# End of layer 0 by image: squares in the scan, attention from the sums of the projection's input, results applied from PSUM

## The chip, the cores and the metric

The kernel runs on one core of a Trainium2 chip. The metric is the device time of one execution in microseconds (us). The program is one launch of about 147,000 instructions on five engines: PE (matmul and, as PEld, its weight loads), DVE (vector), ACT (scalar), POOL (GpSimd) and SP (which here issues DMAs). Each engine works through its own queue of instructions in a fixed order that the framework lays down when the program is built; engines wait for one another with semaphores.

## The reference: what is computed

Four layers run one after the other on an image tensor x of 4 images, 256 channels and 32x32 = 1024 positions (tokens). Layer 0 is a state-space mixer (Mamba-2) with channel attention, layer 1 a non-local block with batch norm, layer 2 attention and a mixture of experts, layer 3 attention and an LSTM of 1024 steps. Everything is float32. The change lies in the end of layer 0, which the reference writes so:

```
y = ys + Dp * xs                                  # output of the scan, per token 256 values
y = y * silu(z)
y = y * rsqrt(mean(y * y, axis=-1) + EPS) * rms_w # RMS norm of each token over its 256 values
out = einsum('bld,ed->ble', y, out_w)             # projection 256 -> 256
out_img = out.transpose to (b, c, h, w)
pooled = mean(out_img over h, w)                  # one number per image and channel
hdn  = relu(pooled @ se1_w.T + se1_b)             # 256 -> 64
attn = sigmoid(hdn @ se2_w.T + se2_b)             # 64 -> 256
x = x + out_img * attn                            # per image and channel
```

Since the projection is linear, the mean of the projected tokens of an image is the projection of the mean of its tokens. The changed kernel uses that.

## The kernel before

The tensor `x` stays in SBUF for the whole program as `s.x`, with channels on the partitions: 2 chunks of 128 channels (`C`), 4 images (`B`), 1024 tokens (`L`). Tokens are handled in tiles of 128 (`NT` = 32 tiles, `TPI` = 8 per image) and in blocks of 512 (`NBLK` = 8 blocks, `BPI` = 2 per image, `TPB` = 4 tiles per block). `_layer0` (L219) normalizes, projects and convolves image by image, computes the decays of the recurrence (`_decays`, L331), and then calls `_scan` (L376) and `_out_and_se` (L439).

`_scan` runs 32 iterations: 8 chunks of 128 tokens outside, 4 images inside, so that all four images end together in the last four iterations. An iteration transposes the inputs on PE into the PSUM tile `ptr` (L395), copies them to SBUF on ACT (`xb`, L398), takes the exponential of the decays on ACT (`m_h`, L409), multiplies on DVE and POOL (L400 to L433), and ends with one DVE multiplication by the gate into `zs[:, n, :]` (L436). ACT has two instructions in an iteration. The scan's PSUM pool holds four names with two buffers each, which is all eight banks.

`_out_and_se` then treats all 32 token tiles together. It squares every tile on ACT and sums along the tokens' 256 values (`sq`, L449), takes one square root over all sums on ACT (L451) and a reciprocal on DVE (L452). Then it goes through the 8 blocks: scale four tiles by `rstd` on DVE (L459), transpose them on PE into `pt`, two chunks of channels of four tiles each (L463), evict `pt` to `yT` on DVE with the multiplication by `rms_w` (L464), project on PE into `po` (L470), and evict `po` to the SBUF tile `o` on ACT, which also sums over the tokens (L473). After the last block follow the two small matmuls of the channel attention for all images (L484, L489), its relu and sigmoid on ACT (L486, L491), and eight DVE instructions of 1024 elements that multiply `o` by the attention and add it to `s.x` (L493). Layer 1 (L499) starts with six small DVE instructions (`theta_wide` and its like, L510) and then matmuls over all of `s.x` (L521).

Who sets the order: the framework's scheduler takes the instructions of the source, and gives each engine an order from priorities (earlier in the source comes first) and from a model of when inputs and buffers are ready; on DVE the instructions of neighbouring iterations of the scan are interleaved in the trace. A tile pool has a number of buffers for each name; when a pool is closed, its memory is given to pools that open later, which then wait until the earlier users are done.

A helper that the change uses exists already: `_rsqrt` (L911) computes 1/sqrt(v + EPS) on DVE alone, by an integer first guess and four Newton steps, sixteen small instructions in all. It is written as a generator, so that callers can mix its steps with others.

## Time and profile before

| | us |
|---|---|
| median of 3 runs | 3567.6 (3564.02 to 3568.08) |
| the profiled execution's own time | 3564.65 |
| its span, first to last instruction | 3562.9 |
| last instruction of the scan (L436) ends | 295.19 |
| first matmul of the output projection (L470) starts | 312.88 |
| last projected block is evicted (L473) | 354.45 |
| first addition to `s.x` (L493) starts | 357.28 |
| first matmul of layer 1 (L521) starts | 367.28 |

The profile gives times from the start of the span. From the end of the scan to the first matmul of layer 1 is 367.28 - 295.19 = 72.1 us, which is 2% of the span. In a view of stretches each row holds, for every engine, its busy us in the stretch and in brackets the number of instructions. In a view of groups each row holds the line of the kernel, the engine, the operation, the tiles it writes and reads, their shapes and the number of instructions; then the busy us and the mean ns of one; and then the time for which the engine stood idle just before these instructions, with what ended it. A float32 matmul shows as two PE records.

### The profile page before, as it was taken

The page shows a single profiled execution, that of the slowest core. Times are in us where ns is not written, and L with a number is a line of the kernel's source. Part 1 is how long each engine was busy: PE and PEld are TensorE (multiplying, and loading weights), DVE is VectorE, ACT ScalarE, POOL GpSimd, SP SyncE. Part 2 cuts the span into 40 slices and gives each one's busy share as a digit, 9 for nine tenths or more (in the row PEclk, how much of TensorE's full clock was granted, in tenths as well). Part 3 has the DMA queues.
Part 4 walks back from the last instruction along what each step waited for, and adds up shares of the span by engine and source line. Part 5 has one row for each costly group of instructions (what it writes and reads, how often), then busy time and mean ns, then how long its engine had stood idle before and what let it go on. Part 6 is the DMA issues. An engine that isn't in the chain of part 4 may idle for free.

```text
span 3562.9 us, 146932 instructions
## 1 busy us (share of the span) xinstructions
PE 3253.3 (91%) x65426; PEld 2549.0 (72%) x65426; DVE 2028.1 (57%) x8373; ACT 1249.5 (35%) x5057; POOL 416.0 (12%) x498
## 2 busy tenths in 40 slices
PE   7786599998899999589999999999999999999888
PEld 4464234445788888357888888888888888888776
DVE  5795544443211111536677777776777777777666
ACT  4623222222222222233334334343343343343333
POOL 0181000113433333200000000000000000000000
PEclk9898789999999999799999999999999999999999
DMA  1390000114455654300000000000000000000000
GB/s 66 88 293 1 9 0 12 36 36 157 175 193 212 223 194 160 125 1 4 5 5 10 4 10 4 5 10 4 4 10 4 10 4 4 10 4 5 10 4 10
DMA packets 79356, 189.32 MB, mean 53 GB/s; under 512 B 6592, under 2 KB 64256, under 8 KB 73728
## 3 DMA queue, kind: packets, MB, share of 16 engines
q0 software_dynamic: 16176, 116.06, 8.9%
q1 hardware_dynamic: 60624, 59.12, 5.6%
q8 instruction: 512, 8.39, 1.0%
q10 hardware_dynamic: 1920, 4.74, 0.4%
q14 instruction: 124, 1.02, 0.1%
HBM read 118.88 MB, written 61.02 MB: 50 GB/s over the span
## 4 chain that ended last, share of the span: by engine, by line
PE 41%; DVE 9%; ACT 4%; issue 2%; ACTq 0%; DVEq 0%
PE p_c L1556 10%; DVE turned L1585 7%; PE p_c L1547 7%; PE p_i L1547 4%; PE p_o L1547 4%; PE p_o L1556 4%; PE p_i L1556 4%; PE beside L1500 4%; ACT a_o L1586 2%; DVE x L1601 2%; ACT th L1599 2%; PE beside L1404 1%; PE beside L1441 0%; PE var L1451 0%; PE p_q L1324 0%
## 5 line engine op out<-in xcount | busy, mean ns | idle before, releaser
L1586 ACT ACTIVATE add<-turned 128x8 f32<-128x8 f32 x1024 | 214.4, 209 | 1027.3 <-DVE turned L1585 1027.3
L1556 PE MATMUL p_c<-w_v,x 128*4 128x64 f32 x16368 | 416.1, 219 | 71.0 <-DVE x L1601 69.0
L1547 PE MATMUL p_c<-xg,shift 128*128 128x64 f32 x2048 | 445.7, 299 | 0.0
L1556 PE MATMUL p_o<-w_v,x 128*4 128x64 f32 x16368 | 416.3, 219 | 0.0
L1556 PE MATMUL p_i<-w_v,x 128*4 128x64 f32 x16368 | 416.1, 219 | 0.0
L1547 PE MATMUL p_i<-xg,shift 128*128 128x64 f32 x2048 | 407.3, 281 | 0.0
L1585 DVE STREAM_TRANSPOSE turned<-p_c 128x64 f32<-128x64 f32 x1024 | 255.7, 250 | 259.0 <-PE p_c L1556 228.0
L1547 PE MATMUL p_o<-xg,shift 128*128 128x64 f32 x2048 | 396.1, 275 | 0.0
L1547 PEld LDWEIGHTS p_c<-xg,shift 128*128 128x128 f32 x2048 | 304.7, 188 | 117.6 <-issue 0.3
L1556 PEld LDWEIGHTS p_c<-w_v,x 128*4 128x4 f32 x16368 | 227.2, 85 | 192.3 <-DVE x L1601 119.1
L1547 PEld LDWEIGHTS p_o<-xg,shift 128*128 128x128 f32 x2048 | 310.9, 192 | 0.3
L1601 DVE TENSOR_TENSOR x<-a_o,th 128x8 f32<-128x8 f32 x1024 | 170.8, 167 | 244.2 <-ACT th L1599 244.2
L1547 PEld LDWEIGHTS p_i<-xg,shift 128*128 128x128 f32 x2048 | 304.7, 188 | 0.4 <-issue 0.3
L1127 PE MATMUL ph<-uT,w 128*128 128x256 f32 x1248 | 282.7, 384 | 16.8 <-DVE uT L1112 12.5
L1141 PE MATMUL po<-w,hT 128*128 128x256 f32 x1248 | 285.5, 382 | 5.6 <-issue 5.0
L1131 ACT ACTIVATE hT<-ph,w 128x256 f32<-128x256 f32 x312 | 147.6, 473 | 398.5 <-PE ph L1127 369.4
L1556 PEld LDWEIGHTS p_o<-w_v,x 128*4 128x4 f32 x16368 | 281.1, 87 | 0.1
L1556 PEld LDWEIGHTS p_i<-w_v,x 128*4 128x4 f32 x16368 | 280.9, 87 | 0.0
L1127 PEld LDWEIGHTS ph<-uT,w 128*128 128x128 f32 x1248 | 238.4, 192 | 54.3 <-DVE uT L1112 16.3
L1585 DVE STREAM_TRANSPOSE turned<-p_i 128x64 f32<-128x64 f32 x1024 | 271.7, 265 | 0.3 <-PE p_i L1547 0.3
L1141 PEld LDWEIGHTS po<-w,hT 128*128 128x128 f32 x1248 | 236.0, 192 | 37.3 <-issue 5.4
L1148 DVE TENSOR_TENSOR y<-po,w 128x256 f32<-128x256 f32 x78 | 33.0, 423 | 392.9 <-PE po L1141 369.6
(409 smaller groups left out, 4678.7 us busy)
## 6 DMA issues: line engine op xcount, KB each, us to landing
sorted<-zeros SPq DMA_DIRECT2D x32, 1032.0 KB
y_in<-results SPq DMA_DIRECT2D x16, 512.0 KB
x<-in_x_dram SPq DMA_DIRECT2D x8, 512.0 KB
tokens<-rows SPq DMA_DIRECT2D x4, 1024.0 KB
x<-tokens SPq DMA_DIRECT2D x8, 512.0 KB
out_dram<-x_l SPq DMA_DIRECT2D x64, 64.0 KB
results<-y,place POOLq DMA_INDIRECT x78
w_l<-in_w_l_dram ACTq DMA_DIRECT2D x1, 1092.0 KB
```

The source lines that it names most:

```text
L1127: nc.tensor.matmul(ph, w1[:, k, bass.ts(n, P)], uT[:, k, :], start=k == 0, stop=k == C - 1,)
L1131: nc.scalar.activation(hT[:, n, :], ph, AF.Gelu, bias=b1[:, n : n + 1])
L1141: nc.tensor.matmul(po, hT[:, n, bass.ts(a, P)], w2[:, n, :], start=n == 0, stop=n == NHC - 1,)
L1148: nc.vector.tensor_add(y, po, b2)
L1404: nc.tensor.matmul(p, lam[:, k, b, bass.ts(m, P)], u_l3[:, k, b * L + n * SB : b * L + (n + 1) * SB], start=k == 0, stop=k == C - 1,)
L1500: nc.tensor.matmul(p[bass.ts(i, R), :], rows[:, k, bass.ts(g, R)], w_u[:, k, at : at + GQ // GC], start=k == 0, stop=k == C - 1, tile_posi ...
L1547: nc.tensor.matmul(p[:, :H], shift[:, row * B : row * B + P], xg[n][:, g, bass.ts(i, H)], start=True, stop=t == 0,)
L1556: nc.tensor.matmul(p[R * i : R * i + B, :H], hs[:, t - 1, bass.ts(k, B)], w_v[:, k, i * GQ + g * H : i * GQ + (g + 1) * H], start=False, s ...
L1585: nc.vector.transpose(zt.rearrange("p c w -> p (c w)"), pz[g][:, :H])
L1586: nc.scalar.activation(dst.rearrange("p (c b) -> p c b", c=C), zt[:, :, :B], f)
L1599: nc.scalar.activation(th, cell[:, :, 1], AF.Tanh)
L1601: nc.vector.tensor_mul(h, a_o, th)
```

## The change

Four things are done differently.

1. The square of each token tile, with its sum, is issued in the scan's iteration right after the gate multiplication, on ACT, into a sum tile `ss` that `_layer0` now holds.
2. The norm's weight `rms_w` is multiplied into the projection's weights once (`wo`), so that the eviction of the transposed tiles no longer carries it. That eviction moves from DVE to ACT and sums over the tokens there (`part`). The scaling by `rstd` is split between ACT (odd tiles) and DVE (even tiles). The root comes from `_rsqrt` on DVE.
3. All work runs image by image. The attention's mean is taken from `part`: reduced and divided on DVE, and sent through `wo` by four small matmuls with one column each (`pooled`), copied to SBUF, and then through the two small matmuls as before, with one column instead of four; the relu is done on DVE.
4. The projection of an image stays in PSUM, in four banks (`po`, 4 buffers), until the attention is there; four DVE instructions of 512 elements read it from PSUM and add it to `s.x`. The tile `o` and its eviction are gone. The PSUM banks are 3 for `pt`, 4 for `po` and 1 for all small matmuls.

```
@@ _layer0
-        _scan(s, xbc, zs, dt, decay, total, tail)
-        _out_and_se(s, zs, w_out, w_se1, se2)
+        ss = keep.tile([P, NT], F32, name="ss")
+        _scan(s, xbc, zs, ss, dt, decay, total, tail)
+        _out_and_se(s, zs, ss, w_out, w_se1, se2)
@@ _scan, end of an iteration
                 nc.vector.tensor_mul(zs[:, n, :], zs[:, n, :], y.rearrange("p h d -> p (h d)"))
+                sq = pool.tile([P, D], F32, name="sq")
+                nc.scalar.activation(sq, zs[:, n, :], AF.Square, accum_out=ss[:, n : n + 1])
@@ _out_and_se
+        ps = ctx.enter_context(tc.tile_pool(name="out_ps", bufs=3, space=PSUM))
+        po = ctx.enter_context(tc.tile_pool(name="out_po", bufs=4, space=PSUM))
+        ps1 = ctx.enter_context(tc.tile_pool(name="out_ps1", bufs=1, space=PSUM))
+        wo = keep.tile([P, C, D], F32, name="wo")
+        for k in range(C):
+            nc.vector.tensor_scalar_mul(
+                wo[:, k, :], w_out[:, k, :], s.col["rms_w"][:, k : k + 1]
+            )
+        small = ps1.tile([P, B, 2 * C + 1], F32, name="small")
+        for b in range(B):
+            ms = pool.tile([P, TPI], F32, name="ms")
+            nc.vector.tensor_scalar_mul(ms, ss[:, bass.ts(b, TPI)], 1.0 / D)
+            rstd = pool.tile([P, TPI], F32, name="rstd")
+            for _ in _rsqrt(s, pool, rstd, ms):
+                pass
+            yT = pool.tile([P, C, L], F32, name="yT")
+            part = pool.tile([P, C, BPI], F32, name="part")
+            for i in range(BPI):
+                for j in range(i * TPB, (i + 1) * TPB):
+                    n = b * TPI + j
+                    if j % 2:
+                        nc.scalar.mul(y[:, n, :], y[:, n, :], rstd[:, j : j + 1])
+                    else:
+                        nc.vector.tensor_scalar_mul(y[:, n, :], y[:, n, :], rstd[:, j : j + 1])
+                for k in range(C):
+                    pt = ps.tile([P, TPB, P], F32, name="pt")
+                    for j in range(TPB):
+                        nc.tensor.transpose(
+                            pt[:, j, :], y[:, b * TPI + i * TPB + j, bass.ts(k, P)], s.ident
+                        )
+                    nc.scalar.activation(
+                        yT[:, k, bass.ts(i, W)], pt.rearrange("p j q -> p (j q)"), AF.Identity,
+                        accum_out=part[:, k, i : i + 1],
+                    )
+            o = [[po.tile([P, W], F32, name="po") for _ in range(BPI)] for _ in range(C)]
+            for m in range(C):
+                for i in range(BPI):
+                    for k in range(C):
+                        nc.tensor.matmul(
+                            o[m][i], wo[:, k, bass.ts(m, P)], yT[:, k, bass.ts(i, W)],
+                            start=k == 0, stop=k == C - 1,
+                        )
+            mean = pool.tile([P, C], F32, name="mean")
+            nc.vector.tensor_reduce(mean, part, AX.X, ALU.add)
+            nc.vector.tensor_scalar_mul(mean, mean, 1.0 / L)
+            pooled, p1, p2 = small[:, b, :C], small[:NSE, b, C : C + 1], small[:, b, C + 1 :]
+            for m in range(C):
+                for k in range(C):
+                    nc.tensor.matmul(
+                        pooled[:, m : m + 1], wo[:, k, bass.ts(m, P)], mean[:, k : k + 1],
+                        start=k == 0, stop=k == C - 1,
+                    )
+            pooled_s = pool.tile([P, C], F32, name="pooled")
+            nc.vector.tensor_copy(pooled_s, pooled)
...
+            nc.vector.tensor_scalar(hdn, p1, s.col["se1_b"][:NSE], 0.0, ALU.add, ALU.max)
+            att = pool.tile([P, C], F32, name="att")
+            for m in range(C):
+                nc.tensor.matmul(
+                    p2[:, m : m + 1], se2[:, bass.ts(m, P)], hdn, start=True, stop=True
+                )
+                nc.scalar.activation(
+                    att[:, m : m + 1], p2[:, m : m + 1], AF.Sigmoid,
+                    bias=s.col["se2_b"][:, m : m + 1],
+                )
             for m in range(C):
+                for i in range(BPI):
+                    xs = s.x[:, m, b, bass.ts(i, W)]
+                    nc.vector.scalar_tensor_tensor(
+                        xs, o[m][i], att[:, m : m + 1], xs, ALU.mult, ALU.add
                     )
```

All lines of the old `_out_and_se` from the square (L449) to the last addition (L493) are replaced by these.

## The prediction

> **What bounds the kernel now.** I read the page's forty slices first, then the table of stretches, the groups and the order of time of the stretch that is changed. The page's chain of waits begins only after 1569 us, so it says nothing here. I take the stretch as serial because everything after it (layers 1 to 3) reads `s.x`, which it writes last; the only other work in flight, the zero-filling DMAs, is down to a DMA share of 0.14 by 260 to 295 us. A microsecond gained before layer 1 should therefore arrive at the end.
>
> The stretches (columns: PE, PEld, DVE, ACT, POOL busy us and counts, granted PE clock, DMA share, GB/s):
>
> ```profile
> 200.00:260.00 60.00, 53.33 (x287) 37.27 (x286) 58.46 (x116) 15.47 (x30) 54.65 (x62) 1.00 1.10 301
> 295.20:310.70 15.50, 0.00 (x0) 0.00 (x0) 0.82 (x3) 14.47 (x66) 0.00 (x0) 0.50 0.00 1
> 310.70:354.50 43.80, 39.38 (x128) 20.25 (x128) 19.29 (x48) 11.00 (x32) 0.00 (x0) 0.93 0.00 0
> 354.50:357.30 2.80, 0.75 (x6) 0.60 (x7) 0.34 (x3) 1.81 (x3) 0.00 (x0) 1.00 0.00 0
> 357.30:367.30 10.00, 0.40 (x3) 0.34 (x3) 10.00 (x11) 0.26 (x1) 0.00 (x0) 0.51 0.26 79
> ```
>
> The first row is the scan: DVE is busy 58.46 of 60 us, ACT only 15.47. In the second row ACT works alone, in the third PE leads, in the last DVE works alone. So of 72.1 us between the scan's end (295.19) and layer 1's first matmul (367.28), 28 us have one engine busy and the others waiting for it.
>
> The groups of that stretch:
>
> ```profile
> L470 PE MATMUL po<-yT,w_l 128*128 128x512 f32 x64 | 31.2, 633 | 3.6 <-DVE yT L464 3.5
> L449 ACT ACTIVATE sq<-zs 128x256 f32<-128x256 f32 x32 | 12.8, 400 | 7.4 <-DVE zs L436 7.4
> L463 PE MATMUL pt<-ident,zs 128*128 128x128 f32 x64 | 9.3, 293 | 17.0 <-DVE zs L459 17.0
> L493 DVE SCALAR_TENSOR_TENSOR x<-o,att,x 128x1024 f32<-128x1024 f32 x8 | 9.7, 1280 | 2.4 <-ACT att L491 2.4
> L451 ACT ACT_TABLE_LOAD x1 | 1.3, 1283 | 0.0
> L491 ACT ACT_TABLE_LOAD x1 | 1.3, 1283 | 0.0
> ```
>
> The squares take 12.8 us, and before the first of them ACT sat idle 7.4 us, although the data of most tiles had long been there: they waited for the scan's very last multiplication. I read that as a wait for memory: a stage of new pools starts only when the scan's pools are free.
>
> The order of time in the scan (start, us, what, idle before):
>
> ```profile
> 268.19 0.60 ACT L409 ACTIVATE m_h<-pd 128x512 f32<-128x512 f32 x1 [3.47 <-PE py L416]
> 268.75 0.48 ACT L398 COPY xb<-ptr 128x384 f32<-128x384 f32 x1
> 269.46 0.74 DVE L436 TENSOR_TENSOR zs<-zs,y 128x256 f32<-128x256 f32 x1
> 272.48 0.60 ACT L409 ACTIVATE m_h<-pd 128x512 f32<-128x512 f32 x1 [3.25 <-PE py L416]
> 294.77 0.42 DVE L436 TENSOR_TENSOR zs<-zs,y 128x256 f32<-128x256 f32 x1
> 295.31 0.42 ACT L449 ACTIVATE sq<-zs 128x256 f32<-128x256 f32 x1 [7.41 <-DVE zs L436]
> ```
>
> Between the copy's end at 269.23 and the exponential at 272.48 ACT idles 3.25 us, and the gate multiplication ends inside that hole, at 270.20. Counted from the end, the copy at 268.75 belongs to iteration 26 and the multiplication at 269.46 to iteration 24: the copies run two iterations ahead.
>
> **What the Trainium skill says.** "ScalarE: Activation LUTs", section "What ACT_TABLE_LOAD costs": about 1283 ns a load; the trace has 1283. The square needs none after the exponential: the trace has no load at 295.31. "TensorE: Matmul & The Clock Gate", Part 1 (the clock gate): an idle window of about 3.4 us puts PE back to half clock, and about 3.4 us of work brings it back. The trace agrees: after 17 us idle the projection's records start 0.85 us apart (312.88 to about 316.9), then 0.43; layer 1's first round takes 7.19 us (367.28 to 374.47), later ones 5.15. Same page, "Architectural detail": ACT and DVE are strict first in, first out. No row tests that alone; rival (c) rests on it.
>
> **The change part by part.** Times are those of the profiled execution.
>
> Scan. 32 squares and accumulator reads move into it, a pitch of 0.40 us each (12.87/32). ACT has the room (26% busy), and the hole shown takes a square without touching the next exponential. In the first half the exponential follows the copy at 0.31 us, and a square put between costs up to 0.4 us on m_h. A reordering by the scheduler can also go either way. Bounds -3 to +8 us; I take +1. Removed from the end are the squares, 12.87, and sqrt, table load and reciprocal (308.18 to 310.20), 2.02.
>
> Start of the new end. The last square after 295.19: 0.7, so 295.9. On DVE `wo` (2 x 0.27, the shape of L459), the mean 0.2, and `_rsqrt`, sixteen instructions, which took 3.09 in the same form (14.13 to 17.22): 3.85, plus 0.6 for the other images' chains mixed in: 300.3. Scaling: 4 instructions on ACT first, each at 0.40 (the page's price 186 + 93 ns for one pointer + 0.833 x 256 less the overlap of 93; L312 with two pointers is 571 ns in the trace), 1.6; the first eviction of 512 columns with its sum, 0.75 (L473's: 0.68): first projection matmul at 302.7. Before it was 312.88.
>
> An image's projection. 16 PE records. The first starts cold: about 4 us at 0.85 (5 records), 11 at 0.43, 9.0 us; ends 311.7.
>
> Attention. The scheduler's priorities follow the source, where the pooled matmuls stand behind the eight projections, so I put them behind: 8 records at 0.11 (L416's pitch) 0.95, copy 0.3, then what lay between `pooled` ready and the first addition before (354.86 to 357.28 = 2.42) less the 0.9 by which the table load was late: 1.5. Sum 2.75. The load itself comes once and stands in front of the sigmoid with nothing to wait for, so it is hidden by the 9 us of projection; uncovered it would cost 0.9 once. Then one addition from PSUM of 0.72 (L530, the same shape with a sum: 0.75) frees the first bank: 3.5 us after the projection's end.
>
> The banks are all taken: 3 + 4 + 1, and the Trainium skill ("PSUM — Partial Sum Buffer", Specifications) gives 8, which the scan's two buffers of four names fill too. The next image's projection thus waits these 3.5 us; its 16 transposes (16 x 0.12 = 1.9) and pooled work fit into the hole. Behind the waiting matmul on PE nothing else is due, and the later banks come free every 0.72, faster than the 1.72 in which one is filled. Period 16 x 0.43 + 3.5 = 10.4; three more images: 342.9. DVE has per image 3.3 + 4 x 0.27 + 0.9 + 4 x 0.7 = 8.1, ACT 4 x 0.40 + 4 x 0.75 + 2 x 0.26 = 5.1: both under the period.
>
> End. 2.75 for the last attention, 4 x 0.72 additions, 0.34 until layer 1's first weights are there: 348.9, where 367.28 was. PE is idle over 3.4 us before, so layer 1's cold start (2.04 us) stays. What is late next is the attention chain, once for each image.
>
> Sum: 348.9 - 367.28 = -18.4, with the scan's +1: -17.4. From 3564.65 that is 3547.2. The profiled execution is 2.95 below the median of the runs (3567.6) and inside their spread; I allow 1 of it: **3548**.
>
> **The rivals.** (a) Better: pooled matmuls find a place in the wait of the bank before, so that the attention is there when an image's projection ends. The period falls to the PE work, 6.9 + 1.9 + 0.9 = 9.7, the last 2.75 go, and PE stays warm for layer 1 (-2): about 26 less, 3539. For it: `part` is ready while the projection runs. Against: source order. (b) Little changes: the scan loses 14 or more (0.45 us an iteration, what the first half's exponentials have no room for, in all 32), and the end wins 18: 3561 and up, 3564 say. DVE's 97% in the scan speaks for it, the 2.7 us mean wait of the exponential in its second half (46.4 us in 17 waits) against. (c) Slower, one mechanism: the square waits at the head of ACT's queue for L436, and the next copy stands behind it. A copy runs 11 us before its own iteration's gate (268.75 to 279.8, iteration 26), 2.7 iterations of 4.06. If the squares held ACT so that only two iterations were under way, the period would be 11.7/2 = 5.9, +1.8 x 32 = 58, less 18: 3605. It decides from 0.58 us an iteration (18.4/32). For it: the queue's order. Against: the scheduler places by readiness, as DVE's mixed order shows, so a square stands where its input was due. (d) Memory is given back tile by tile and image 0 starts during the scan's last 8 us, where DVE and ACT idle: 8 more, 3540. The 7.41 us wait speaks against.
>
> **How the numbers follow.** Forecast 0.62, (a) and (d) together 0.20, (b) 0.10, (c) 0.08. The forecast's own range with the scan's bounds (-4 to +7 round its +1) and 4 us for mixed queues: 3540 to 3559. Reaching to the better rivals: 3536 to 3560. A measurement here tells about 0.2%, 7 us, from no change. Faster by more than that: 0.62 + 0.20 and a little of (b), 0.83; within: 0.08; slower: 0.09.
>
> **What would show it.** Right: no row of 32 squares after the scan; the scan's last multiplication near 296; first projection near 303; PE gaps of about 3.5 us between four groups of 16 records, ended by DVE's addition; layer 1 near 349. Wrong: copies (L398) that wait for DVE's gate, a scan over 310, table loads inside the scan (64 loads of 1.28 would be +82), or a period over 12 us for an image.

## The result and the profile after

| | before | after |
|---|---|---|
| median, us | 3565.81 (3560.08 to 3568.08) | 3543.13 (3540.56 to 3545.86, 4 runs) |
| profiled execution's own time | 3564.65 | 3545.86 |
| its span | 3562.9 | 3544.2 |
| last gate multiplication of the scan ends | 295.19 | 294.77 |
| first matmul of the projection | 312.88 | 302.73 |
| first matmul of layer 1 | 367.28 | 351.31 |
| from the scan's end to layer 1 | 72.1 | 56.5 |

The changed kernel is faster: ratio 0.9942, 95% interval 0.993 to 0.9953, that is 16.8 to 25.0 us of 3565.8. The profiled executions differ by 18.8 us, of which 16.0 have been won when layer 1 begins. The other 2.8 arise behind it, where both kernels issue the same instructions; they come back further down.

Line numbers are those of the changed kernel: two more than before in the scan, 28 more behind layer 0. The stretches of the changed kernel, with the columns of the table before (PE, PEld, DVE, ACT, POOL busy us and counts, granted PE clock, DMA share, GB/s):

```profile
200.00:260.00 60.00, 54.12 (x290) 38.00 (x288) 58.61 (x119) 23.22 (x62) 55.18 (x62) 1.00 1.09 302
294.80:299.30 4.50, 0.01 (x1) 0.04 (x1) 3.63 (x31) 0.96 (x4) 0.00 (x0) 0.50 0.00 0
299.30:302.70 3.40, 3.40 (x16) 3.37 (x17) 3.26 (x23) 3.25 (x10) 0.00 (x0) 0.50 0.00 0
302.70:310.00 7.30, 7.30 (x20) 3.36 (x19) 6.03 (x34) 5.41 (x15) 0.00 (x0) 0.96 0.00 0
310.00:315.10 5.10, 4.32 (x37) 3.63 (x35) 1.35 (x4) 3.25 (x8) 0.00 (x0) 1.00 0.00 0
...
322.10:326.40 4.30, 4.30 (x38) 3.76 (x37) 1.87 (x5) 2.83 (x9) 0.00 (x0) 1.00 0.00 0
...
337.00:345.80 8.80, 8.80 (x18) 3.87 (x19) 2.15 (x5) 0.05 (x1) 0.00 (x0) 0.81 0.00 0
345.80:351.30 5.50, 1.96 (x17) 1.62 (x15) 3.34 (x8) 0.52 (x2) 0.00 (x0) 0.98 0.26 58
```

The first row is the scan: ACT's busy time has gone from 15.47 to 23.22 of 60 us, DVE's from 58.46 to 58.61. The squares are in and DVE, the busiest engine of the scan, does as much in the stretch as before. Then come the root (DVE alone, 4.5 us), image 0's transposes at half clock (3.4 us), its projection (7.3 us), and what lies between the projections of two images. Those stretches aren't empty: in the second of them PE is busy for 4.30 of 4.30 us.

The groups between 290 and 352 us (line, engine, operation, tiles, shapes and count, then busy us, mean ns, idle time before and what ended it):

```profile
L488 PE MATMUL po<-yT,wo 128*128 128x512 f32 x64 | 30.2, 628 | 0.4 <-DVE x L522 0.4
...
L477 PE MATMUL pt<-ident,zs 128*128 128x128 f32 x64 | 11.2, 319 | 6.4 <-DVE zs L473 6.2 <-ACT yT L480 0.2
L522 DVE SCALAR_TENSOR_TENSOR x<-po,att,x 128x512 f32<-128x512 f32 x16 | 10.9, 743 | 5.2 <-ACT att L515 5.2
...
L515 ACT ACT_TABLE_LOAD x1 | 1.3, 1283 | 0.0
```

The projection (31.2 us before) and the additions (9.7 before, 10.9 now from PSUM) cost what they did. The additions lie beside PE's work now, except the last four. In all four images the projection waited for an addition for 0.4 us: the idle column of the first row is the first sign that the wait for a bank is a small part of what lies between two projections.

### The profile page after: what moved, and what is told of

Same layout as the page of the kernel before. It is cut to its first block, busy times and chain, and to the rows that moved or that the text cites. A ratio compares the mean times of both kernels' runs of the same rounds, so it can differ in the third digit from the quotient of the medians.

```text
span 3544.2 us, 147127 instructions
## 1 busy us (share of the span) xinstructions
PE 3255.7 (92%) x65482; PEld 2557.6 (72%) x65482; DVE 2027.0 (57%) x8432; ACT 1256.9 (35%) x5076; POOL 416.4 (12%) x498
## 4 chain that ended last, share of the span: by engine, by line
PE 41%; DVE 9%; ACT 4%; issue 2%; ACTq 0%; DVEq 0%
PE p_c L1584 11%; DVE turned L1613 7%; PE p_c L1575 7%; PE p_i L1575 4%; PE p_o L1575 4%; PE p_i L1584 4%; PE p_o L1584 4%; PE beside L1528 4%; ACT a_o L1614 2%; DVE x L1629 2%; ACT th L1627 2%; PE beside L1432 1%; PE beside L1469 0%; PE var L1479 0%; PE p_q L1352 0%
## 5 line engine op out<-in xcount | busy, mean ns | idle before, releaser
L1613 DVE STREAM_TRANSPOSE turned<-p_o 128x64 f32<-128x64 f32 x1024 | 255.9, 250 | 0.1
```

Source lines behind the costliest of these rows:

```text
L1613: nc.vector.transpose(zt.rearrange("p c w -> p (c w)"), pz[g][:, :H])
```

## The experiments

The distances in the table are from the end of the scan's last gate multiplication to layer 1's first matmul. The distances of 53.1 and 51.4 that two of the expectations below start from were read from that multiplication's start, 0.42 earlier.

| kernel | scan ends | first projection | layer 1 begins | distance | time, us | ratio |
|---|---|---|---|---|---|---|
| before | 295.2 | 312.9 | 367.3 | 72.1 | 3565.8 | |
| after | 294.8 | 302.7 | 351.3 | 56.5 | 3543.1 | 0.993 to 0.9953 |
| after, again | 294.7 | 302.7 | 351.2 | 56.5 | 3545.8 | 0.9938 to 0.9965 |
| squares in one row | 297.7 | 314.0 | 361.2 | 63.5 | 3558.3, 1 run | |
| squares by image | 295.9 | 306.6 | 352.6 | 56.7 | 3546.5, 1 run | |
| squares alone | 294.6 | 299.9 | 353.4 | 58.8 | 3551.0 | 0.9937 to 0.997 |
| sigmoid at the head | 296.2 | 304.2 | 351.7 | 55.5 | 3548.2, 1 run | |
| sigmoid after the scan | 295.7 | 303.7 | 350.5 | 54.8 | 3547.4, 1 run | |
| squares in line | 412.1 | 420.2 | 467.7 | 55.5 | 3663.3, 1 run | |
| attention first | 297.0 | 305.0 | 349.7 | 52.7 | 3540.0 | 0.9924 to 0.9951 |
| attention first, again | 295.2 | 303.1 | 347.5 | 52.3 | 3548.3 | 0.9933 to 0.996 |
| folded | 294.7 | 305.0 | 345.6 | 51.0 | 3539.5 | 0.9907 to 0.9935 |
| roots by image | 296.5 | 305.1 | 346.2 | 49.7 | 3540.0 | 0.9912 to 0.9939 |

The scan's end differs by 1.9 us between two executions of one kernel (attention first), so differences of that size in it mean nothing. That is why I compare distances. Each distance is that of one profiled execution; the two executions of the changed kernel agree to 0.1 us, those of attention first to 0.4.

**Squares out of the scan, in one row.** The changed kernel with the squares where they were:

```
@@ _scan
-                sq = pool.tile([P, D], F32, name="sq")
-                nc.scalar.activation(sq, zs[:, n, :], AF.Square, accum_out=ss[:, n : n + 1])
@@ _out_and_se, ahead of the loop over images
+        for n in range(NT):
+            sq = pool.tile([P, D], F32, name="sq")
+            nc.scalar.activation(sq, y[:, n, :], AF.Square, accum_out=ss[:, n : n + 1])
```

> The changed kernel with its 32 squares taken out of the scan and put in one row in front of the first image. Marks in the changed kernel's trace: the scan's last gate multiplication ends at 294.77 us, ACT's first scaling is at 298.84, layer 1's first matmul at 351.31. Theory A (the squares are free inside the scan, and their price outside is ACT's queue): the scan ends within 0.5 us of 294.8; 32 squares at 0.40 hold ACT until about 307.6; DVE's root for image 0 hides behind them, so everything after is late by 307.6 - 298.8 = 8.8 us, not by 12.9; layer 1 at about 360, the whole about 3555. Theory B (the squares cost time inside the scan): the scan ends at 293 or earlier, and layer 1 comes at 358 or earlier.

The time was 3558.31, the distance 63.5, 7.0 more than the changed kernel's. The scan ended 2.9 us later although it had no squares to do. So no price that the scan pays for them is to be seen. Theory A had the distance right (8.8 us more, 8.7 measured when the fall of the clock that the next paragraph names is left out), but not the scan's end. The first square, in the order of time:

```profile
297.82 0.42 ACT L459 ACTIVATE sq<-zs 128x256 f32<-128x256 f32 x1 [7.79 <-DVE zs L438]
```

It waits 7.79 us for the last gate multiplication, as it waited 7.41 before. In this form the row of squares is on the path, for 7.0 of its 12.8 us, or 8.7 without the clock's fall. The other 4.1 are the time for which ACT waits for the root in the changed kernel (294.77 to 298.84); here the root's instructions on DVE lie beside the squares.

**Squares out of the scan, image by image.** The same, with the eight squares of an image at the head of its turn:

```
         for b in range(B):
+            for n in range(b * TPI, (b + 1) * TPI):
+                sq = pool.tile([P, D], F32, name="sq")
+                nc.scalar.activation(sq, y[:, n, :], AF.Square, accum_out=ss[:, n : n + 1])
```

> The changed kernel with the squares taken out of the scan and put at the head of each image, eight for each. Theory A (only what stands in front of the first image is exposed; the other images' squares go into ACT's gaps, 5.1 + 3.2 = 8.3 us of work in a period of 10.6 to 12.4): 8 x 0.40 = 3.2 us later than the changed kernel, layer 1 at about 354.5, the whole about 3549. Rival (ACT's queue is what paces an image, since it also does the evictions): each image grows by up to 3.2 us, layer 1 at 361 to 364, the whole 3556 or more.

The time was 3546.54, the distance 56.7, as good as the changed kernel's 56.5 within what one profile tells. The first projection comes 3.8 us later (306.57 against 302.73), or 2.7 counted from the scan's end, because image 0's root starts only behind its eight squares: 3.4 us after the scan's end (299.33) where it was 0.6 (295.40). Of that, 1.7 come back because this execution's last projection took 7.13 us where the changed kernel's took 8.83, which is the clock and not the squares, and 0.9 because the first two periods are shorter (11.62 and 11.17 against 12.37 and 11.28; the cause is open). Without that fall of the clock the changed kernel's distance would be 54.8, and squares by image cost 1.9 us more than squares in the scan, less than theory A's 3.2 and far from its rival's.

**Squares in the scan, and nothing else.** The kernel before with its 32 squares moved into the scan:

```
@@ _scan
+                sq = pool.tile([P, D], F32, name="sq")
+                nc.scalar.activation(sq, zs[:, n, :], AF.Square, accum_out=ss[:, n : n + 1])
@@ _out_and_se
-        ss = keep.tile([P, NT], F32, name="ss")
-        for n in range(NT):
-            sq = pool.tile([P, D], F32, name="sq")
-            nc.scalar.activation(sq, y[:, n, :], AF.Square, accum_out=ss[:, n : n + 1])
```

> The kernel before with the squares moved into the scan and nothing else changed: root on ACT, blocks, eviction to SBUF, attention at the end. Theory A (most of the gain is the row of squares): of 12.9 us the last square (0.6) stays, so layer 1's first matmul comes at 367.28 - 12.3 = 355.0, the whole 12.3 us under the kernel before, about 3552; working by image and applying from PSUM would then be worth only 355.0 - 351.3 = 3.7 us. Rival (the gain comes from the whole rebuild, and the scan pays for the squares): layer 1 at 360 or later.

The median was 3550.97 (3549.17 to 3552.66), ratio 0.9953 with the interval 0.9937 to 0.997; the distance fell from 72.1 to 58.8. That is theory A, with 1.0 us more than it priced: the first eight records of the projection took 4.44 us here and 5.54 before, since PE's full clock came 1.5 us after their start and not 3.7. As times of the whole program, this kernel and the changed one can't be told apart by their intervals (0.9937 to 0.997 and 0.993 to 0.9953); the profile tells them apart by 2.2 us at layer 1's start. Its stretches after the scan:

```profile
299.90:340.50 40.60, 36.25 (x120) 18.41 (x120) 17.02 (x40) 10.98 (x32) 0.00 (x0) 0.98 0.00 0
340.50:343.50 3.00, 0.88 (x7) 0.73 (x7) 0.49 (x3) 1.83 (x4) 0.00 (x0) 0.82 0.00 0
343.50:353.40 9.90, 0.51 (x3) 0.45 (x3) 9.90 (x11) 0.26 (x1) 0.00 (x0) 0.50 0.26 80
```

The projection takes 40.6 us, then 3 us of attention, then 9.9 us in which DVE works alone: the old end, started earlier. Set beside the two runs above, the parts don't add up:

| | squares behind the scan | squares in the scan |
|---|---|---|
| old end | 72.1 | 58.8 |
| new end | 63.5 in one row, 56.7 by image | 56.5 |

With the old end the squares are worth 13.3 us. With the new end, which would do them for one image while PE projects another, they are worth 7.0 in one row and 0.2 by image (8.7 and 1.9 without the clock's fall). The other way about, the new end is worth 8.6 us without the squares' move (squares in one row) and 2.2 (3.9 without the fall) with it. The parts of the new end (the root on DVE, the eviction on ACT, the projection kept in PSUM, the work by image) weren't tried one by one; what each is worth stays open.

**The squares made to stand in line.** One order by hand on ACT: the copy of an iteration (L400) only after the square of the iteration before.

```
-                nc.scalar.copy(xb, ptr[:, :3, :])
+                copied = nc.scalar.copy(xb, ptr[:, :3, :])
+                if c + b > 0:
+                    tc.add_manual_dep(
+                        copied.ins, squared.ins.name,
...
-                nc.scalar.activation(sq, zs[:, n, :], AF.Square, accum_out=ss[:, n : n + 1])
+                squared = nc.scalar.activation(sq, zs[:, n, :], AF.Square, accum_out=ss[:, n : n + 1])
```

> The changed kernel with one order written by hand: on ScalarE each scan iteration's copy comes only after the square of the iteration before it. This is the case of the prediction's rival in which squares stand ahead of the next copy. My theory (iterations of the scan overlap, and their square slides between the next copy and the next exponential at no cost): with the overlap forbidden an iteration takes its whole chain from copy to gate, 7.3 us, and 0.7 us of square, 8 us in place of about 4; the scan ends some 125 us later, the whole about 3670. The rival's own price was 58 us: about 3605. A third case: no change over 5 us, if iterations hardly overlap.

The time was 3663.25, the scan ended 117 us later, the distance stayed (55.5). An iteration in the order of time:

```profile
256.36 0.42 ACT L448 ACTIVATE sq<-zs 128x256 f32<-128x256 f32 x1 [1.22 <-DVE zs L446]
256.69 0.19 ACT L448 ACTIVATION_READ_ACCUMULATOR sq<-zs 128x1 f32 x1
256.78 0.46 ACT L400 COPY xb<-ptr 128x384 f32<-128x384 f32 x1
...
262.77 0.60 ACT L419 ACTIVATE m_h<-pd 128x512 f32<-128x512 f32 x1 [5.54 <-PE py L426]
...
264.08 0.42 DVE L446 TENSOR_TENSOR zs<-zs,y 128x256 f32<-128x256 f32 x1
...
264.59 0.42 ACT L448 ACTIVATE sq<-zs 128x256 f32<-128x256 f32 x1 [1.22 <-DVE zs L446]
```

From square to square it is 8.23 us: copy, a wait of 5.54 for the matmuls, exponential, gate, and again the square. In the changed kernel the same instructions stand so (from 277 us):

```profile
277.32 0.63 DVE L438 TENSOR_TENSOR zs<-zs,y 128x256 f32<-128x256 f32 x1
278.04 0.42 ACT L440 ACTIVATE sq<-zs 128x256 f32<-128x256 f32 x1 [1.28 <-DVE zs L438]
278.36 0.19 ACT L440 ACTIVATION_READ_ACCUMULATOR sq<-zs 128x1 f32 x1
279.47 0.48 ACT L400 COPY xb<-ptr 128x384 f32<-128x384 f32 x1 [0.92 <-POOL y L421]
280.22 0.60 ACT L411 ACTIVATE m_h<-pd 128x512 f32<-128x512 f32 x1 [0.28 <-PE py L418]
```

The square is there too in front of a copy, but it is the square of an older iteration, and the copy waits for something else (0.92 us, for POOL). The danger of the prediction's rival (c) is real and dearer than it priced it: not two iterations under way, but one. PE's granted clock fell too, to 0.77 and 0.69 in two stretches of 60 us, where it was 1.00; how much of the 117 us that is wasn't tried.

**The table load early.** A sigmoid of a constant at the head of the new end, to draw the load ahead:

```
+        warm = keep.tile([P, 1], F32, name="warm")
+        nc.scalar.activation(warm, s.eps, AF.Sigmoid)
```

> The changed kernel with one sigmoid of a constant column on ACT right behind the scan, so that the sigmoid's table is loaded while DVE computes the root. In the changed kernel the load stands at 312.53, 0.6 us after the matmuls that the first sigmoid reads, and the hole on PE between the first and the second image's projection is 5.1 us against 4.3 and 3.6 later. Theory A (the load is late for the first image by what it takes less 0.4): the hole shrinks to about 4.1, layer 1 at about 350.2, the whole 1.1 us less. Rival (the hole is paced by the transposes and evictions of the second image, which fill it): no change beyond 0.3 us.

A miss: the instruction depends on nothing, and the framework placed it inside the scan. The table was loaded at 286.66, the exponential's table again at 288.57, and the sigmoid's once more at 314.58 for the real gate. The stretch after image 0's projection stayed at 5.07 us.

**The table load after the scan.** The same with an input that holds it back:

```
+        nc.scalar.activation(warm, ss[:, NT - 1 :], AF.Sigmoid)
```

> The changed kernel with one sigmoid more, of one of the squares' sums, so that ScalarE can load the sigmoid's table only when the scan's last square is done. My theory: the table load of 1.3 us then lies beside the root's chain and not in the first image's attention chain, the hole in the first projection after image 0 falls from 5.1 to about 4 us, and layer 1 begins about 1 us nearer to the scan's end (55.5 in place of 56.5). Rival: the hole is filled with transposes and evictions that have to be done anyway; the load's place changes the distance by less than 0.3 us, or adds to it because it delays ScalarE's first scalings.

In the order of time:

```profile
296.32 1.28 ACT L460 ACT_TABLE_LOAD   x1
...
303.67 8.18 PE L490 MATMUL po<-yT,wo 128*128 128x512 f32 x16
...
316.00 1.45 PE L490 MATMUL po<-yT,wo 128*128 128x512 f32 x3
```

The load lies under the root. Between the end of image 0's projection and the start of image 1's there are now 4.15 us (311.85 to 316.00) in place of 5.08 (310.02 to 315.10), so the load had cost 0.9. The distance fell by 1.7. This doesn't follow from the load alone: image 0's projection took 0.9 longer (8.18 against 7.29) and the last image's 1.7 less (7.13 against 8.83), both with the granted clock. In the kernel with the load inside the scan these two projections took 7.93 and 7.13; its stretch didn't shrink, and its distance fell by 1.1 all the same.

**The attention written ahead of the projection.** The eight projection matmuls of each image moved behind mean, gate and sigmoid in the source, and nothing else:

```
-            o = [[po.tile([P, W], F32, name="po") for _ in range(BPI)] for _ in range(C)]
-            for m in range(C):
...
             mean = pool.tile([P, C], F32, name="mean")
...
                     bias=s.col["se2_b"][:, m : m + 1],
                 )
+            o = [[po.tile([P, W], F32, name="po") for _ in range(BPI)] for _ in range(C)]
+            for m in range(C):
...
```

> The changed kernel with each image's mean, pooled matmuls, gate network and attention written before its projection instead of after it. My theory: the 3.6 to 5.1 us between an image's last first projection matmul and its first result addition are the attention chain standing behind the projection only because it was written behind it. Then that chain lies under the projection: no 2.7 us chain after the last image, a period of about 10.6 us (projection 7, transposes 1.9, small matmuls 1.6) or less, and 49 to 52 us from the end of the scan to layer 1's first matmul in place of 56.5; the whole 3536 to 3541. Rival (TensorE is the bound there anyway): the small matmuls now stand between the projection's, wait for their own chain there and hold the projection up; the period stays at 11 or more, the distance at 55 or more, the whole within 3 us of the changed kernel's.

And on another chip, beside the kernel after it:

> The kernel with the attention written before the projection, again, beside the one above on the same chip: 53 us from the scan's last gate multiplication to layer 1's first matmul, a period of 11.2 to 11.3 us, the median between 3538 and 3543. If it lies within 1 us of the changed kernel's two medians (3543.1 and 3545.8), the place of the attention is worth less than the runs can tell.

The stretches of the second of the two runs, one for each image and one for layer 1's start:

```profile
303.10:312.80 9.70, 9.70 (x35) 4.74 (x34) 8.02 (x38) 7.20 (x18) 0.00 (x0) 0.96 0.00 0
312.80:324.00 11.20, 11.20 (x50) 6.20 (x49) 3.87 (x9) 2.95 (x10) 0.00 (x0) 1.00 0.01 1
324.00:335.20 11.20, 11.20 (x49) 6.14 (x48) 3.60 (x8) 2.94 (x10) 0.00 (x0) 1.00 0.00 0
335.20:346.50 11.30, 11.30 (x49) 6.04 (x47) 4.55 (x14) 2.95 (x10) 0.00 (x0) 1.00 0.13 31
346.50:352.00 5.50, 4.66 (x12) 2.15 (x12) 0.91 (x3) 1.37 (x2) 0.00 (x0) 1.00 0.21 84
```

PE is never idle in the four stretches of the images, and the period is 11.2 us all the same, as in the changed kernel (12.37, 11.28, 10.61). That is the rival's side of the first question. My theory's sum of 10.6 us for PE's work lacked a term, which the order of time shows:

```profile
317.19 1.10 PE L515 MATMUL po<-yT,wo 128*128 128x512 f32 x2
318.23 0.39 PE L497 MATMUL small<-pooled,w_l 128*64 128x1 f32 x4
```

Two projection records between small matmuls take 1.04 to 1.06 us from start to start, and 0.86 in a row. An image's 16 records so take 7.55 us in place of 6.87, without a wait in the profile.

Of the 3.8 to 4.2 us by which the distance fell, 1.7 are again the fall of the clock that the changed kernel met in its last projection and this one didn't. The other 2.1 to 2.5 come from the end, where no chain stands behind the last image. That is my theory's side of the second question, though the distances of 52.7 and 52.3 miss its 49 to 52. Behind that mark, layer 1's first four records take 1.98 us where the changed kernel's took 3.53, since PE arrives at full clock. The median was 3540.02 in the first comparison and 3548.29 in the second, where 3538 to 3543 had been expected (ratios 0.9937 and 0.9946). Against the changed kernel's two ratios this is no difference that the runs can tell, though layer 1 begins 3.8 us nearer to the scan's end.

**The same with less work for PE.** The first matmul of the gate network is multiplied with the projection's weights once, so that an image's eight `pooled` matmuls and their copy go:

```
+        pw = ps.tile([P, C, C, P], F32, name="pt")
...
+                nc.tensor.transpose(pw[:, k, m, :], w_out[:, k, bass.ts(m, P)], s.ident)
+        nc.scalar.copy(woT, pw)
...
+                nc.tensor.matmul(
+                    pf[:, k, :NSE], woT[:, k, m, :], w_se1[:, m, :],
...
-                        pooled[:, m : m + 1], wo[:, k, bass.ts(m, P)], mean[:, k : k + 1],
...
-                    p1, w_se1[:, k, :], pooled_s[:, k : k + 1], start=k == 0, stop=k == C - 1
+                    p1, wf[:, k, :], mean[:, k : k + 1], start=k == 0, stop=k == C - 1
```

> The kernel with the attention written before the projection, and in it the output projection and the gate network's first matrix multiplied together once (4 transposes and 4 small matmuls, in TensorE's idle time under the root's chain at the scan's end), so that the 8 pooled matmuls of each image and their copy fall away. My theory (with the attention in front, TensorE's own work sets the 11.25 us per image): the period falls by the 0.8 to 0.95 us of the 8 records to 10.3 to 10.5, layer 1's first matmul comes 49 to 50.5 us after the scan's last gate multiplication in place of 53.1, and the whole falls 3 to 4 us below the kernel with the attention in front, to 3536 to 3537. Rival (the chain of mean, gate and sigmoid, or DVE's additions that free the banks, sets the period): it stays at 11 or more, with TensorE idle where the records were, and the distance stays above 52. A third: the extra matmuls at the head delay image 0 by up to 2 us and give the half of it back.

Its stretches for the second and third image:

```profile
313.70:324.00 10.30, 10.30 (x42) 5.40 (x41) 5.25 (x15) 4.53 (x14) 0.00 (x0) 1.00 0.01 2
324.00:334.30 10.30, 10.30 (x42) 5.34 (x41) 3.49 (x7) 2.94 (x10) 0.00 (x0) 1.00 0.00 0
```

The period falls by 0.9 us, the time of the records that are gone, and PE is still busy all the time. So PE's own work sets the period. The third case came true as well: the small products and their evictions stand among the root's instructions on DVE, the first projection begins 10.3 us after the scan in place of 8.0, and the distance falls by 1.3 to 1.7, not 3.5. The median was 3539.50, 8.8 below the kernel above on the same chip, and its ratio of 0.9921 (0.9907 to 0.9935) is the best of all, below the changed kernel's 0.9942 and 0.9951, though the intervals of the first two still touch. The expected 3536 to 3537 weren't reached. The two profiled executions differ by 5.9 us, of which only 1.8 (345.64 against 347.46) stand at layer 1's start; why the rest came behind it isn't known.

**The root of an image as soon as its squares are there.** The sums get a tile for each image, and the root's tiles lie in memory set aside before the scan:

```
-        ss = keep.tile([P, NT], F32, name="ss")
+        ss = [keep.tile([P, TPI], F32, name=f"ss{b}") for b in range(B)]
+        roots = ctx.enter_context(tc.tile_pool(name="l0_roots", bufs=B))
...
-            ms = pool.tile([P, TPI], F32, name="ms")
+            ms = roots.tile([P, TPI], F32, name="ms")
```

> The folded kernel with the squares' sums of each image in a tile of its own and the root's tiles in memory that is set aside before the scan, so that image 0's root need not wait for the last image's square nor for the scan's memory. This tries the prediction's rival (d). My theory: the root began only after the scan's last square because it read one tile that all squares write and lay in memory given back by the scan; now it begins before the scan's last gate multiplication, image 0's first scaling comes 3 to 5 us after that multiplication in place of 6.8, layer 1's first matmul 48 to 50 us after it in place of 51.4, and the whole is 1.5 to 3 us less, 3536 to 3538. Rival (DVE takes the four images' chains mixed, so image 0's scaling waits for the last image's sums all the same): first scaling no nearer than 6 us, distance above 50.7, no change of the whole. In a third case the root's small instructions delay the scan's last steps, and its end comes 1 us later.

In the order of time:

```profile
295.46 0.23 DVE L479 TENSOR_SCALAR ms<-ss 128x8 f32<-128x8 f32 x2
...
296.08 0.41 DVE L439 TENSOR_TENSOR zs<-zs,y 128x256 f32<-128x256 f32 x1
...
301.66 1.31 ACT L489 ACTIVATE zs<-zs,rstd 128x256 f32<-128x256 f32 x3 [3.90 <-DVE rstd L972]
```

The root begins before the scan's last gate multiplication now, so one tile for all sums, or the memory, had indeed held it; which of the two wasn't tried alone. Image 0's first scaling comes 5.2 us after that multiplication's end in place of 6.4 (5.6 and 6.8 from its start; my theory had 3 to 5), the distance is 49.7 in place of 51.0. DVE still takes the images' chains and the small products mixed. The median, 3539.98, isn't below the folded kernel's, and the 3536 to 3538 of my theory weren't reached.

**The changed kernel again.**

> The changed kernel again, unaltered. If the profiled gain of 18.7 us is made of 16 us up to layer 1 and some 2.7 us that come and go in the later stages with their transfers, layer 1 begins at 351 plus or minus 1.5 again while the later stages' share of the gain differs by a us or more; the median lies between 3541 and 3546. If the later share is a consequence of the change, it is there again with the same 2 to 3 us.

Layer 1 began at 351.23, where the first execution has 351.31. The median was 3545.80 (3544.58 to 3548.09) and the ratio 0.9951, interval 0.9938 to 0.9965. So the two executions of the changed kernel agree, and the larger figure of 22.7 us between the medians of the first comparison is at the upper side of what the runs give: 17.8 in the second.

**The 2.8 us behind layer 1.** Of these, 2.4 lie in one stretch, from the start of layer 3 to its query projection: 113.7 us before, 111.3 after. One group of it before, and then the same one after:

```profile
L1287 PE MATMUL p_u<-kt,rows 128*128 128x256 f32 x128 | 35.2, 423 | 1.3 <-DVE kt L1285 1.3
```

```profile
L1315 PE MATMUL p_u<-kt,rows 128*128 128x256 f32 x128 | 33.6, 408 | 1.3 <-DVE kt L1313 1.3
```

The same 128 records take 423 and 408 ns, at a granted clock of 0.95 (1495.7 to 1581.3 us) and 0.98 (1477.5 to 1560.8). In the two executions of the kernel with the attention first they took 422 and 405, again at 0.95 and 0.98, and the stretch 115.3 and 111.1. So a difference of this size comes and goes with the clock of an execution. That the change has no part in it isn't shown: from layer 1's start to the end it is 3195.7 us before and 3192.9 in both executions of the changed kernel, which is the side that the expectation had given to a consequence of the change. But there is only one profiled execution of before, over all kernels this remainder lies between 3192.1 and 3196.2, and between the two executions of attention first it differs by 1.9. The 16.0 us up to layer 1 are the part that the profile explains.

## Why the prediction was right

It said 3548.0, a gain of 17.4 in the profiled execution, and named the mechanism: squares under the scan, one image's end beside the next one's work. The time came out at 3543.1, and at 3545.8 in the second comparison. The sum was nearer than its terms, which is partly luck: at layer 1's start, as far as it reasoned, the gain in the profile was 16.0 where it had 17.4, and the stages behind added 2.8 that it hadn't foreseen.

**Scan, +1 (bounds -3 to +8).** It ended 0.42 us earlier, and the executions scatter by more than that. The squares took holes of ACT, as the prediction read from one hole.

**Start, first projection at 302.7.** It came at 302.73, but two terms missed and cancelled. The scaling began at 298.84 and not at 300.3: the root's chain began at 295.40 and not at 295.9, `wo` was made before the scan's end (293.49 and 294.08; 0.54 had been priced), and the other images' chains cost 0.4 less than allowed. And the transposes, which the prediction gave no time of their own beside the scaling and one eviction, took 3.65 us at half clock (299.29 to 302.94).

**"A stage of new pools starts only when the scan's pools are free."** Too broad. `wo`, in a new pool, ran before the scan's last gate multiplication, while squares in a new pool waited 7.79 and 7.63 us for it. With other tiles the root began earlier too. Some of the memory is given back earlier, as rival (d) had it; it isn't worth 8 us, because image 0's chain on DVE is mixed with the others.

**Image 0's projection, 9.0 us, cold.** It took 7.29: only its first 0.5 us were at half clock. The transposes ahead of it had kept PE busy for 3.65 us, and the full clock was back at 303.26. How soon it comes back is in part chance: in the other kernels with the new end this was 0.3 to 2.3 us after the first projection's start (in the kernel with the table load after the scan 2.3, and the projection took 8.18). Before the change it took 5.9 us of work on PE (310.74 to 316.62), more than the "about 3.4" that the prediction read there.

**Hole of 3.5 us after each image, ended by DVE's addition.** This is the step that failed. The holes were 5.08, 4.25 and 3.58 us, 12.9 in place of 10.5, and for the most part they were no holes. The first of them in the changed kernel, and the marks of the two others:

```profile
302.73 7.29 PE L488 MATMUL po<-yT,wo 128*128 128x512 f32 x16
309.87 0.95 PE L498 MATMUL small<-mean,wo 128*128 128x1 f32 x8
310.68 0.53 PE L477 MATMUL pt<-ident,zs 128*128 128x128 f32 x3
...
312.24 1.31 PE L477 MATMUL pt<-ident,zs 128*128 128x128 f32 x10
312.53 1.28 ACT L515 ACT_TABLE_LOAD   x1
...
314.12 2.07 DVE L522 SCALAR_TENSOR_TENSOR x<-po,att,x 128x512 f32<-128x512 f32 x3 [2.35 <-ACT att L515]
314.14 0.38 PE L512 MATMUL small<-hdn,se 64*128 64x1 f32 x2 [0.58 <-ACT att L515]
314.71 0.55 PE L477 MATMUL pt<-ident,zs 128*128 128x128 f32 x3 [0.20 <-ACT yT L480]
315.10 1.45 PE L488 MATMUL po<-yT,wo 128*128 128x512 f32 x3
...
324.90 2.73 DVE L522 SCALAR_TENSOR_TENSOR x<-po,att,x 128x512 f32<-128x512 f32 x4 [1.03 <-ACT att L515]
325.68 0.87 PE L477 MATMUL pt<-ident,zs 128*128 128x128 f32 x6
326.38 7.03 PE L488 MATMUL po<-yT,wo 128*128 128x512 f32 x16
...
336.19 2.73 DVE L522 SCALAR_TENSOR_TENSOR x<-po,att,x 128x512 f32<-128x512 f32 x4 [1.03 <-ACT att L515]
```

PE does the gate network's matmuls (0.95 + 0.39 + 2 x 0.38) and the transposes of later images there: 19, 20 and 9 of them in the three holes, 16 an image. The chain itself came as priced: behind the second and third projection (ended at 322.13 and 333.41) the first addition starts after 2.77 and 2.78 us, where the prediction had 2.75, and frees its bank after 3.5. But in the second hole PE is then still at its own instructions, for 0.75 us more. In the third, where seven of the transposes had been done before, it waits 0.40 us for the addition, and only there the hole is what the prediction described. What it had wrong is that 16 transposes and the small matmuls "fit into the hole". From start to start, 20 transposes take 2.65 us in the second hole and the small matmuls 1.76, so with 16 transposes (2.1 by the same rate, an estimate) PE needs 3.9 us from its first small matmul on, where the bank is free 3.7 us after the same mark (321.97 to 325.63). They don't fit into the hole, they fill it.

The term is "16 x 0.43 + 3.5 = 10.4"; it measured 11.4 in the mean (12.37, 11.28, 10.61). Its reason was the attention chain where PE's own instructions were the limit: in all of the second hole and all but 0.4 us of the third. In the first the chain still decided 0.8 us, through the table load. Rival (a) called a period of 9.7 PE's work and left out p1 and p2 (1.15 us). The attention in front showed the bound: no wait left, period 11.2, though 0.7 of that is the price of its own order; and folding showed it again: 0.9 less work, 0.9 less period. The first period is also over the 12 us that the prediction had named as a sign of being wrong. Table load and half clock explain it: without these 0.9 and 0.3 us it is 11.2.

**Table load "hidden".** Not hidden: it stood behind an eviction in ACT's order and came at 312.53, when the gate's input was there. Moving it shortened that stretch by 0.9, the size that the prediction named for the case.

**Projections at 0.43 a record.** The middle two took 7.0 us, as priced. The last took 8.8 in both executions of the changed kernel, and 7.1 in the five other kernels with the new end that write the projection ahead of the attention. The stretches about it:

```profile
333.98:337.39 3.41, 2.97 (x20) 2.19 (x21) 1.57 (x4) 2.37 (x8) 0.00 (x0) 1.00 0.00 0
337.39:340.81 3.42, 3.42 (x5) 1.35 (x4) 1.76 (x5) 0.00 (x0) 0.00 (x0) 0.50 0.00 0
```

For 3.41 us the clock is at half, 1.7 us that no step of the prediction had. The Trainium skill ("TensorE: Matmul & The Clock Gate", Part 1) speaks of an activity window of about 3.4 us that runs freely. The traces agree: in each of them the changes of the clock lie a whole number of times 3.413 us apart, here at 303.26, ten steps later at 337.39, and at 340.81. So it matters how this grid falls on PE's work. In the changed kernel a step begins 0.40 us after the last projection's start, in its second execution 0.38 us after; the 3.41 us before it hold transposes, small matmuls, 0.44 us of idle time and only 0.4 us of projection. Four other kernels issue the same PE instructions there with the same wait (squares in one row, sigmoid at the head, sigmoid after the scan, squares in line). Their grid lies 0.77 to 2.20 us after that start, and their clock doesn't fall. So the order of instructions doesn't decide it alone. That the grid's place does is what the figures suggest; no experiment moved it on purpose, and how much work a step must hold isn't known.

**End, 2.75 + 4 x 0.72 + 0.34 to layer 1.** From the last projection's end it took 5.5, not 6.0. Layer 1's start at half clock stayed, as said: 3.53 us for its first four records.

So at layer 1 the terms miss by -1.7 (cold start), +2.4 (holes), +2.25 (projections, mostly clock) and -0.5 (end): +2.4 in all, 351.3 against 348.9.

**The rivals.** (a) was right that PE would be the bound and that the chain at the end could go; it needed another order in the source, and gave 2.1 to 2.5 us by layer 1's start (without the clock's fall) and 1.6 in its first records, not 9. (b) didn't happen. (c) happened when the order was forced: +117 us in the scan, where it had priced 58, because the forced order left one iteration under way and the rival had reckoned with two. (d) is worth 1.3 us as far as it was tried.

## What to carry to other kernels

When work is put in the gaps of an engine that isn't the bound, ask whose input it waits for and what its queue holds behind it: the same 32 squares cost nothing that the runs can tell where the scheduler could place them behind the next iteration's copy, and 117 us where they stood in front of it. Before pricing a wait between two blocks, add up everything that the waiting engine has to issue in that time; if the sum fills the wait, the wait isn't the bound, and shortening the chain buys only the last occurrence and a start at full clock. The sum isn't free of the order either: here mixing small matmuls into a projection made it 0.7 us longer. And two changes that use the same overlap don't add: here 13.3 and 8.6 us apart made 15.5 together (17.2 without the clock's fall).

## What the runs showed of the hardware that was not expected

- Transposes count for the clock here: after about 6 us idle, 16 of them (3.65 us at a granted clock of 0.50) and 0.5 us of projection were followed by the full clock from 303.26 us on, and from 310.09 to 313.50 us PE did transposes and one-column matmuls alone and kept a clock of 1.00.
- The granted clock changes in steps: in all thirteen traces its changes lie whole multiples of 3.413 us apart, on a grid that isn't tied to the program's start (counted back in whole steps, it lies 2.7 us behind it in one execution of attention first and on it in the other). One step at half clock (337.39 to 340.81) cost the last projection 1.7 us in the changed kernel; other kernels with the same PE instructions there met none.
- Matmuls with one column are not free: eight float32 records of one column took 0.95 us, and taking them out shortened the period by 0.9. Two 512-column records set between them took 1.04 to 1.06 us, 0.86 in a row.
